# Layer 1's keys-times-values product on half of the columns, with the halves exchanged by transfers

## The chip, the cores and the metric

The kernel runs on one core of a Trainium2 chip. The metric is the device time of one execution in microseconds; the time of a version is the median of its runs. Engines are called PE (TensorE, matrix products), DVE (VectorE), ACT (ScalarE), POOL (GpSimd) and SP (SyncE, which here only issues transfers).

## The reference, cut to what matters

The program applies four layers to an array of 4 images x 512 channels x 1024 positions, all in f32: an attention of 8 heads (layer 0), a linear attention (layer 1), an attention of one head over a layer norm (layer 2), and an attention of 4 heads over a group norm (layer 3). The change is in layer 1:

```python
V = einsum('bcn,oc->bon', xf, wv) + bv          # 512 channels
V = gate * V                                    # gate: max + mean over positions
Qf, Kf = softplus(Q), softplus(K)               # 64 features each
KV = einsum('bmn,bcn->bmc', Kf, V)              # 64 x 512
norm = 1 / einsum('bnm,bm->bn', Qf, sum(Kf) + EPS)
wval = einsum('bnm,bmc,bn->bcn', Qf, KV, norm)
out = x + gamma * wval
```

The kernel never forms V. Since V is linear in x, it computes (Kf x^T) first, a 64 x 512 matrix for each image, and multiplies that by wv^T. This second product, of (64 x 512) by (512 x 512), plus bv times the sums of the keys, is the matrix `kv` that the change touches.

## The kernel before, in words

Channels lie on the 128 partitions in four chunks (`NC = 4`); positions are handled in two blocks of 512 (`NTB = 2`). Images go through each layer one after the other. Every f32 product of the source is two records of PE in the profile.

PE's instructions run in the order in which the program issues them (a manual schedule for that engine alone). The order on DVE, ACT, POOL and SP is chosen by a planner from priorities and its own estimates of times; `soon()` raises a priority.

Layer 1 of an image is cut into pieces, the list that `linear_attention` returns at its end, and these are filled into the large products of other work. `slot()` stands between those products: each call takes the next piece from the list `pieces` and issues it. For the first three images the other work is layer 0's projection of the next image (`project_qkv`): 11 slots among its first products, then 7 in `project_v`, so that 18 slots stand against 16 pieces. `flush()` issues what remains. For the last image the pieces lie among layer 2's weight products (6 slots), its first projection (7), `project_v` (7) and `one_head` (10), together with layer-norm pieces, and one more piece after them that writes the updated image to memory (`away`) and loads another (`back`). `project_v` and `one_head` are both built by `seven_products`, a scheme of seven products in place of eight, whose results DVE joins with additions (lines 746, 783, 789).

The pieces that matter here come in this order. `keys_times_x` (line 1493) forms Kf x^T in two halves of 64 rows, one from even and one from odd blocks of positions. `divide_queries` divides the query features by the norm. `transpose_kx` transposes the result, copies it from PSUM by ACT (`kxh`), and adds the two halves of 64 columns by DVE into `kxt`, once for each of two copies, so that `kxt` has 128 columns of which the second 64 repeat the first. `keys_times_values` multiplies by wv: four products (one for each chunk of channels), 128 columns wide, so that the 64 rows of the result stand twice in `kv`, on partitions 0 to 63 and 64 to 127. Both copies are needed, because `update` multiplies the lower half of the partitions with the first block of positions and the upper half with the second, side by side. The feature tile `feat` and `kv` live in one buffer, which the profile names `block`. After an empty piece (`idle`), `update(0)` and `update(1)` each fill two PSUM tiles of the pool that also holds attention's scores (two buffers), and DVE adds them to x, 128x1024 at a time (line 1558).

Small tiles of 128x512 come from `row_tile`, which has three buffers.

Of the kernel before, what the change touches and what calls it, by code (L numbers as in the profile page):

```python
# [15 lines left out]
ALU = mybir.AluOpType  # L16
# [6 lines left out]
NC = C // P  # L23
# [4 lines left out]
M = 64  # L28
# [447 lines left out]
def plain_path(ctx: ExitStack, tc: tile.TileContext, d: dict, out: bass.AP, count):  # L476
# [11 lines left out]
    nc = tc.nc  # L488
# [11 lines left out]
    def acc_tile():  # L500
        return ps_acc.tile([P, TB], F32, tag="acc", name="acc")

    def two_tile(name):
        return ps_sc.tile([P, 2, TB], F32, tag="sc", name=name)

    def row_tile(name):
        return work.tile([P, TB], F32, tag="row", bufs=3, name=name)
# [18 lines left out]
    def chunks_tile(tag, name, bufs=1):  # L526
        return work.tile([P, NC, TB], F32, tag=tag, bufs=bufs, name=name)
# [71 lines left out]
    wv1 = chunks_tile("xn", "wv1", 2)  # L599
# [8 lines left out]
    kv = block1[:, 3, :]  # L608
    bv1 = const.tile([P, C], F32, name="bv1")
# [37 lines left out]
    def product(ps, lhs, rhs):  # L647

        for c in range(NC):
            nc.tensor.matmul(ps, lhsT=lhs(c), rhs=rhs(c), start=(c == 0), stop=(c == NC - 1))  # L650
# [751 lines left out]
    def linear_attention(b, scratch):  # L1402

        x = xs[b]
        t = {}
        flat = lambda tile: tile.rearrange("p a s -> p (a s)")
        half = lambda h: slice(h * M, (h + 1) * M)
# [119 lines left out]
        def transpose_kx():  # L1527
            ps = two_tile("kxt")[:, 0, :]
            for c in range(NC):
                nc.tensor.transpose(ps[:, bass.ts(c, P)], t["kx"][:, bass.ts(c, P)], ident)  # L1530
            halves = row_tile("kxh")
            nc.scalar.copy(halves, ps)
            h = halves.rearrange("p (c a m) -> p c a m", c=NC, m=M)
            kxt = t["kxt"] = row_tile("kxt").rearrange("p (c a m) -> p c a m", c=NC, m=M)
            for a in range(2):
                nc.vector.tensor_tensor(
                    kxt[:, :, a, :], h[:, :, 0, :], h[:, :, 1, :], ALU.add
                )

        def keys_times_values():  # L1540

            ps = two_tile("kv")[:, 0, :]
            product(
                ps, lambda c: t["kxt"][:, c].rearrange("p a m -> p (a m)"), lambda c: wv1[:, c, :]
            )
            nc.vector.scalar_tensor_tensor(kv, bv1, t["kcol"], ps, ALU.mult, ALU.add)

        def update(a):

            for o in (2 * a, 2 * a + 1):  # L1550
                ps = two_tile("upd")
                for tb in range(NTB):
                    nc.tensor.matmul(  # L1553
                        ps[:, tb, :], lhsT=kv[half(tb), bass.ts(o, P)],
                        rhs=feat[half(tb), bass.ts(tb, TB)], start=True, stop=True,
                    )
                xv = x[:, o, :]
                nc.vector.scalar_tensor_tensor(
                    xv, flat(ps), t["gate"][:, o : o + 1], xv, ALU.mult, ALU.add
                )  # L1560
# [11 lines left out]
            both(lambda: keys_times_x(2), lambda: keys_times_x(3), sum_keys),  # L1572
            divide_queries,
            transpose_kx,
            keys_times_values,
            idle,
            *[lambda a=a: update(a) for a in range(NC // 2)],
        ]

# [109 lines left out]
    with tc.manual_schedule(engines={mybir.EngineType.PE}):  # L1689
# [8 lines left out]
        for b in range(B):  # L1698
            vt = v_tiles()
            if b > 0:  # L1700
                pieces.extend(linear_attention(b - 1, lambda i: vt[i]))
            q, k = project_qkv(
                wqkv0, "bqkv0", lambda tb: xs[b][:, :, bass.ts(tb, TB)], vt,
                lambda: chunks_tile("ot", "ws"), first=(b == 0),
                between=outputs_bias,
            )
            flush()
            if b > 0:
                away(b - 1)
                if b + 1 < B:  # L1710
                    nc.sync.dma_start(x_tile(b + 1), xin[b + 1])
                else:
                    back(0)
            if b == 0:
                os = output_sums(wo0)
            if b == B - 1:
                w2 = wpool.tile([P, 3 * NC, C], F32, tag="wqkv", name="w2")
                nc.sync.dma_start(w2, d["w2"].rearrange("(c p) o -> p c o", p=P))
            attention(
                b, q, lambda c, j: k[:, c, bass.ts(j, P)], vt, 8, 64.0**-0.5, wo0, os, bo0[0],  # L1720
                plain=(b == B - 1),
            )
# [31 lines left out]
        flush()  # L1754
        wo2 = load_wo(d["wo2"])
        lin = linear_attention(B - 1, lambda i: pt_tile("l1"))

        norms[1][0]()
# [4 lines left out]
        for o in range(NC):  # L1763
            ps = gps.get(o)
            if ps is None:
                ps = acc_tile()
# [5 lines left out]
        for o in range(NC):  # L1772
            ps = acc_tile()
# [11 lines left out]
        for b in range(B):  # L1785
# [9 lines left out]
            half = NC // 2  # L1795
# [156 lines left out]
```

## Time and profile before

| | before |
|---|---|
| median of 3 runs | 2435.08 us (2434.74 to 2436.24) |
| profiled execution | 2434.68 us |
| its span, first to last instruction | 2433.0 us |
| PE busy | 2416.0 us (99%) |
| DVE busy | 1497.2 us (62%) |
| ACT busy | 697.6 us (29%) |
| POOL busy | 250.8 us (10%) |
| kv products (line 650), 32 records | 592 ns median of one |
| kxt additions, 128x256, 8 | 419 ns median of one |
| kv = bv * sum + product, 128x512, 4 (line 1546) | 748 ns median of one |
| granted TensorE clock | 1.000 |

The table's times of single instructions are durations on their engine. Products on PE are pipelined: a new record of 512 columns starts long before 592 ns have passed, so that the length of a stage on PE is to be read from where it starts and where the next one starts, not from the sum of its records. The chain of waits lists the work that set the end, in order of time, and is the view for this. In lists of DVE, ACT and SP by time, the bracket at the end of a line is the idle time just before the instruction and what ended it.

### The profile page before, as it was taken

Reading aid. Unit: us, or ns where it says so; the run is one execution under the profiler, and the core shown is the slowest. Engines: PE = TensorE matmul, PEld = TensorE weight load, DVE = VectorE, ACT = ScalarE, POOL = GpSimd, SP = SyncE. Lnnn points to the kernel's source line nnn. Section 1 sums busy time; section 2 is a strip of 40 time slices with the busy share of each in tenths; the row PEclk is TensorE's granted clock in tenths of the full one; section 3 lists DMA queues with packets and bytes.
Section 4 is the critical chain, followed back from the end, with each engine's and each line's share of the span. In section 5 each row is a group of like instructions: output and inputs, shape, how many; then the busy total and the mean of one; then the engine's idle time right before and its main releaser. Section 6 shows DMA issues by size and latency. Waiting matters only on the chain.

```text
span 2433.0 us, 24544 instructions
## 1 busy us (share of the span) xinstructions
PE 2416.0 (99%) x10002; PEld 1203.5 (49%) x10002; DVE 1497.2 (62%) x1786; ACT 697.6 (29%) x860; POOL 250.8 (10%) x240
## 2 busy tenths in 40 slices
PE   9999999999999999999999999999999999999999
PEld 4444544453455344544646446455556446555653
DVE  3678577757875789556595775754453554445344
ACT  1454154406431643121211302013321330322132
POOL 4001100110020002102103021021020001002000
PEclk9999999999999999999999999999999999999999
DMA  5001120211022121111001020110110011001001
GB/s 186 9 11 42 46 79 17 55 61 44 19 77 87 58 58 53 44 52 69 1 0 69 5 87 0 52 70 18 35 70 0 18 35 52 1 35 35 1 22 45
DMA packets 41900, 104.35 MB, mean 43 GB/s; under 512 B 3419, under 2 KB 19291, under 8 KB 38838
## 3 DMA queue, kind: packets, MB, share of 16 engines
q1 hardware_dynamic: 41782, 102.73, 12.5%
q8 instruction: 80, 1.31, 0.2%
q14 instruction: 38, 0.31, 0.0%
HBM read 68.98 MB, written 33.74 MB: 42 GB/s over the span
## 4 chain that ended last, share of the span: by engine, by line
PE 98%; DVE 1%; ACT 1%; issue 0%; DMA 0%; SPq 0%; DVEq 0%
PE acc L716 19%; PE acc L841 12%; PE acc L976 9%; PE acc L991 9%; PE sc L945 9%; PE sc L940 9%; PE acc L848 8%; PE acc L1093 7%; PE acc L1325 6%; PE acc L1286 2%; PE acc L1027 1%; PE acc L650 1%; PE upd L1553 1%; PE acc L1493 1%; PE kv L650 1%; PE feat L650 1%
## 5 line engine op out<-in xcount | busy, mean ns | idle before, releaser
L950 ACT ACTIVATE pt<-sc 128x1024 f32<-128x1024 f32 x384 | 379.2, 1022 | 541.2 <-PE sc L945 304.0
L959 DVE TENSOR_TENSOR sum<-sum,pt 128x1024 f32<-128x1024 f32 x256 | 314.4, 1228 | 159.3 <-ACT pt L950 147.2
L976 PE MATMUL acc<-pt,v 64*64 64x512 f32 x2048 | 248.4, 591 | 0.0
L940 PE MATMUL sc<-q,k 64*64 64x512 f32 x2048 | 245.5, 591 | 1.1 <-ACT pt L950 1.1
L991 PE MATMUL acc<-pt,v 128*128 128x512 f32 x512 | 240.8, 594 | 0.0
L945 PE MATMUL sc<-q,k 128*128 128x512 f32 x512 | 239.8, 593 | 0.0
L716 PE MATMUL acc<-t,ws 128*128 128x512 f32 x384 | 173.9, 593 | 0.0
L704 POOL TENSOR_TENSOR ws<-wqkv 128x256 f32<-128x256 f32 (+1 forms) x40 | 39.2, 981 | 1296.7 <-PE acc L1027 516.1
L956 DVE TENSOR_TENSOR sum<-pt 128x1024 f32<-128x1024 f32 x64 | 78.0, 1219 | 137.4 <-ACT pt L950 137.4
L991 PEld LDWEIGHTS acc<-pt,v 128*128 128x128 f32 x512 | 96.6, 190 | 125.3 <-issue 121.6
L945 PEld LDWEIGHTS sc<-q,k 128*128 128x128 f32 x512 | 96.8, 190 | 116.2 <-issue 93.1
L976 PEld LDWEIGHTS acc<-pt,v 64*64 64x64 f32 x2048 | 77.5, 133 | 143.9 <-issue 141.1
L940 PEld LDWEIGHTS sc<-q,k 64*64 64x64 f32 x2048 | 76.9, 133 | 141.8 <-issue 132.9
L716 PEld LDWEIGHTS acc<-t,ws 128*128 128x128 f32 x384 | 72.7, 190 | 88.0 <-issue 87.3
L755 ACT COPY v<-acc 128x512 f32<-128x512 f32 x24 | 14.0, 585 | 305.2 <-PE acc L841 305.2
L687 DVE RECIPROCAL rd<-acc 128x512 f32<-128x512 f32 (+1 forms) x24 | 80.5, 3353 | 29.1 <-PE acc L1027 29.1
L841 PE MATMUL acc<-ws,t 128*128 128x256 f32 x384 | 86.8, 379 | 0.0
L848 PE MATMUL acc<-qs,w 128*128 128x512 f32 x192 | 86.3, 592 | 0.0
L848 PE MATMUL acc<-q,ln 128*128 128x512 f32 x192 | 85.8, 593 | 0.0
L1093 PE MATMUL acc<-ot,wo 128*128 128x256 f32 x336 | 80.6, 383 | 2.7 <-ACT ou L1112 2.7
L746 DVE TENSOR_TENSOR v<-acc,v 128x512 f32<-128x512 f32 x72 | 49.6, 690 | 53.7 <-PE acc L841 53.6
L755 ACT COPY q<-acc 128x512 f32<-128x512 f32 x40 | 23.4, 585 | 195.8 <-PE acc L716 195.8
(323 smaller groups left out, 3420.1 us busy)
## 6 DMA issues: line engine op xcount, KB each, us to landing
home<-x SPq DMA_DIRECT2D x8, 2048.0 KB
x<-home SPq DMA_DIRECT2D x8, 2048.0 KB
squares<-squares SPq DMA_DIRECT2D x32, 256.0 KB
out<-x SPq DMA_DIRECT2D x32, 256.0 KB
rds<-quotients SPq DMA_DIRECT2D x30, 256.0 KB
rds<-quotients SPq DMA_DIRECT2D x7, 1024.0 KB
x<-in_x SPq DMA_DIRECT2D x3, 2048.0 KB
v<-squares SPq DMA_DIRECT2D x12, 512.0 KB
```

The lines of the kernel that those rows point to most:

```text
L687: nc.vector.reciprocal(rd, ps)
L716: nc.tensor.matmul(ps, lhsT=w[:, m, :], rhs=x[:, m, :], start=start, stop=stop, skip_group_check=True)
L841: nc.tensor.matmul(ps[:, bass.ts(r, C // 2)], lhsT=x[:, m, bass.ts(2 * o + r, P)], rhs=w[:, m, :], start=(start and r == 0), stop=stop, sk ...
L848: nc.tensor.matmul(ps, lhsT=x[:, m, bass.ts(o, P)], rhs=w[:, m, :], start=start, stop=stop, skip_group_check=True,)
L940: nc.tensor.matmul(ps[half(h), s, :], lhsT=key(g, i)[half(s), half(h)], rhs=q[qb][half(s), g, :], start=True, stop=True,)
L945: nc.tensor.matmul(ps[:, s, :], lhsT=key(g, 2 * i + s), rhs=q[qb][:, g, :], start=True, stop=True)
L950: exps.append(nc.scalar.activation(pt, ps, AF.Exp, scale=scale).ins)
L959: adds.append(nc.vector.tensor_tensor(acc, acc, pt, ALU.add).ins)
L976: nc.tensor.matmul(outs[qb, g][r][half(s), :], lhsT=v[i // 2][half(r), i % 2, g * P + s * hd : g * P + (s + 1) * hd], rhs=pt[half(r), s, : ...
L991: nc.tensor.matmul(outs[qb, g][0], lhsT=v[j // 2][:, j % 2, bass.ts(g, P)], rhs=pt[:, s, :], start=(j == 0), stop=(j == NT - 1),)
L1093: nc.tensor.matmul(ps[i][:, bass.ts(o, n)], lhsT=w[:, m, bass.ts(o, P)], rhs=t[:, m, :], start=(start and m + o == 0), stop=(stop and m == ...
L1325: nc.tensor.matmul(ps[i, o], lhsT=w[m][:, bass.ts(o, P)], rhs=t[m], start=(start and m == 0), stop=(stop and m == 3), skip_group_check=True,)
```

## The change

`kxt` keeps one copy of 64 columns. `keys_times_values` now issues four products of 64 columns: chunks 0 and 1 of the channels accumulate into the lower half of the partitions, chunks 2 and 3 into the upper half, in alternation. Each half thus holds a partial sum over half of the channels. ACT copies both from PSUM into a tile `own`. Two transfers on SP write `own`'s upper half to the lower half of a second tile `other`, and its lower half to the upper half. DVE forms bv times the keys' sum plus `own`, and a new piece, `add_halves`, adds `other`, so that both halves of `kv` again hold the full sum. The new piece stands behind the empty one, so that the list has 17 pieces and both updates are one slot later.

```diff
-            kxt = t["kxt"] = row_tile("kxt").rearrange("p (c a m) -> p c a m", c=NC, m=M)
-            for a in range(2):
-                nc.vector.tensor_tensor(
-                    kxt[:, :, a, :], h[:, :, 0, :], h[:, :, 1, :], ALU.add
-                )
+            t["kxt"] = row_tile("kxt")[:, : NC * M].rearrange("p (c m) -> p c m", m=M)
+            nc.vector.tensor_tensor(t["kxt"], h[:, :, 0, :], h[:, :, 1, :], ALU.add)
 
         def keys_times_values():
 
             ps = two_tile("kv")[:, 0, :]
-            product(
-                ps, lambda c: t["kxt"][:, c].rearrange("p a m -> p (a m)"), lambda c: wv1[:, c, :]
-            )
-            nc.vector.scalar_tensor_tensor(kv, bv1, t["kcol"], ps, ALU.mult, ALU.add)
+            for i, h in itertools.product(range(NC // 2), range(2)):
+                c = h * NC // 2 + i
+                nc.tensor.matmul(
+                    ps[half(h), :], lhsT=t["kxt"][:, c, :], rhs=wv1[:, c, :],
+                    start=(i == 0), stop=(i == NC // 2 - 1),
+                )
+            own = row_tile("kv")
+            nc.scalar.copy(own, ps)
+            other = t["other"] = row_tile("kv")
+            for h in range(2):
+                nc.sync.dma_start(other[half(h)], own[half(1 - h)])
+            nc.vector.scalar_tensor_tensor(kv, bv1, t["kcol"], own, ALU.mult, ALU.add)
+
+        def add_halves():
+
+            nc.vector.tensor_tensor(kv, kv, t["other"], ALU.add)
...
             transpose_kx,
             keys_times_values,
             idle,
+            add_halves,
             *[lambda a=a: update(a) for a in range(NC // 2)],
```

## The prediction

> **What bounds the kernel now.** I read the busy times first, then the chain of waits over the whole run, then the same chain in two stretches around the edited stage, then VectorE's and SyncE's instructions in order of time. On the page:
>
> ```profile
> PE 2416.0 (99%) x10002; PEld 1203.5 (49%) x10002; DVE 1497.2 (62%) x1786; ACT 697.6 (29%) x860; POOL 250.8 (10%) x240
> ...
> PE 98%; DVE 1%; ACT 1%; issue 0%; DMA 0%; SPq 0%; DVEq 0%
> ```
>
> TensorE is busy 2416.0 of 2433.0 us and is 98% of the chain. So time taken off TensorE comes off the end, as long as nothing new makes TensorE wait. The chain around the edited stage of the first image (start, us, what; an f32 product is two records, so x8 is four products):
>
> ```profile
> 268.19 1.87 PE acc L1493 x8
> 270.05 3.63 PE acc L716 x8
> 273.68 1.87 PE acc L1493 x8
> ...
> 284.50 3.46 PE acc L841 x16
> 287.95 3.43 PE kv L650 x8
> 291.39 6.91 PE acc L841 x32
> 298.29 1.92 PE upd L1553 x8
> 300.21 3.65 PE acc L841 x16
> 303.86 1.92 PE upd L1553 x8
> 305.78 7.10 PE acc L841 x32
> ```
>
> The edited product (kv) takes 3.43 us between two stretches of other products without a gap. keys_times_x (L1493) has four products of the same moving size, each filling 64 columns of the array and alternating between its two halves: 1.87 us. The pieces stand one slot (x16, about 3.43 us) apart. The last image is alike:
>
> ```profile
> 1011.42 3.56 PE kv L650 x8
> 1014.98 6.91 PE acc L841 x32
> 1021.89 1.92 PE upd L1553 x8
> 1023.81 3.65 PE acc L841 x16
> 1027.46 1.92 PE upd L1553 x8
> ```
>
> **What the Trainium skill says.** "TensorEngine Tiling (Array Packing)", section Theoretical Speedup: up to 2x when the stationary operand has at most 64 columns. The trace agrees: 1.87 against 3.43 us. Its section Key Properties says that a change of tiling mode drains TensorE. The trace agrees again: from one L1493 stage to the next is 273.68 - 268.19 = 5.49 us, and the eight full-width records between are worth 3.43, so the narrow stage costs 2.06 us, against a bare half of 3.43, 1.72: about 0.35 us for both switches. "DMA: Bandwidth & Descriptors", section Anatomy of one DMA, gives about 2.0 us fixed per transfer plus bytes over 436 GB/s, fitted for another issue path; the trace has 1.77 us from the issue of a quotients transfer of 8 KB (210.54) to the issue of the read that waits for it (212.31), so the fixed part is of that order.
>
> **The change part by part.**
>
> 1. TensorE, keys_times_values. Removed: four full-width products per image, 3.43 us, and the 32 records after them take 6.91 where 4 x 1.72 = 6.88 (eights of them start at 1016.55, 1018.27 and 1020.00): 3.46 us together (last image 3.56 + 0.03 = 3.59). Added: four half-width products in the L1493 form (128 rows, 64 columns, 512 moving, different moving data in the two halves, as there), with full-width records on both sides: 2.06 us. Gain 3 x 1.40 + 1.53 = **5.7 us**. Bounds: if the two switches cost nothing, 3 x 1.74 + 1.87 = 7.1; if the halves did not overlap, -4 x 0.35 = -1.4.
>
> 2. kxt: one addition of 128x256 (0.42 us) instead of two. VectorE ended the second at 286.01, TensorE read it at 287.8: hidden in three images.
>
> 3. ACT: one copy of 128x512 from PSUM added, 0.59 us by the kxh copy. ACT is otherwise idle for 24.09 us before the attention's first exponential (beyond a 1.28 us table load). Hidden; a copy late by 1 us only makes the transfer late by 1 us.
>
> 4. The transfers: two of 64 partitions x 2 KB = 128 KB each on SP, 0.35 to 0.6 us per issue. The trace of before shows none between two places in SBUF. Low bound 1.8 us (the 8 KB one), high bound 6.3 us (the 2 MB write home, 1031.07 to 1037.39). I take 1.77 + 0.35 for the second issue + 256 KB at about 400 GB/s (0.65) = 2.8 us. SP waits for the ACT copy; behind it on SP stands only the write home of x at 307.47, which waits for the updates anyway.
>
> 5. VectorE: the scalar_tensor_tensor now reads SBUF (0.75 as before) and one addition of 0.69 us is new. Counting from the start of kv: products end at 1.9, copy 2.6, transfers 5.4, addition 6.2. The first update reads kv at 2.06 + 3 slots x 3.43 = 12.4. Cover: 6 us; even the high bound of 6.3 ends at 9.7. The addition is in VectorE's queue ahead of the joins of project_v (0.69 each, and idle 1.04 between):
>
> ```profile
> 291.43 0.75 DVE L1546 SCALAR_TENSOR_TENSOR block<-bv,kcol,kv 128x512 f32<-128x512 f32 x1 [5.41 <-PE kv L650]
> 293.15 0.69 DVE L783 TENSOR_TENSOR v<-v,acc 128x512 f32<-128x512 f32 x1 [0.98 <-PE acc L841]
> 294.88 0.69 DVE L789 TENSOR_TENSOR v<-v,acc 128x512 f32<-128x512 f32 x1 [1.04 <-PE acc L841]
> ```
>
> If it waits there for the transfer, the joins behind it are late; TensorE needs the first of them three products (5.2 us) later, so a wait under about 3 us costs nothing. I take 0; bounds 0 and 3 us an image.
>
> 6. The extra piece. Both updates come one slot later. In the first three images 18 slots take 16 pieces now and 17 after, so no remainder is run in a block; 7.10 us (two slots) between the last update and the scores become one. The scores take the two PSUM buffers that the update used; VectorE's two update additions end 3.7 us after the update's start, the scores come at 1.92 + 3.63 = 5.5: cover 1.9 us, cost 0. The next x, loaded after the write home (307.47, 313.86), comes about 2 us later and is read more than 100 us later.
>
> 7. In the last image the 20 slots before one_head are full. The second update moves into one_head, behind its first ten products: from 1027.5 to about 1029.4 - 1.5 - 2.1 + 13.8 + 3.4 = 1043. Its own price on TensorE is the same. With it goes the round trip of x:
>
> ```profile
> 1031.07 0.34 SPq L574 DMA_DIRECT2D home<-x  x1
> 1037.39 0.34 SPq L577 DMA_DIRECT2D x<-home  x1
> ...
> 1047.38 0.68 DVE L1588 TENSOR_TENSOR s<-x 128x512 f32<-128x512 f32 x1
> ```
>
> Write 6.3 us, read until about 1044.6 (DMA goes idle between 1043 and 1045): 13.5 us. After the change: updates done 1046.8, home 1053.2, back 1060.4, three additions (2.1 us). The lnsums product that reads them comes at 1077.48 - 1.5 = 1076. Cover 13 us: cost 0. Without cover: see the second rival. VectorE's additions for it now fall where joins and exponential sums keep it full (1057.7 to 1064.7 almost without a gap): 0 to 2 us, I take 0.
>
> **Sum.** -5.7 + 0 = -5.7 us. On the profiled execution: 2434.68 (span 2433.0 and 1.7 around it) becomes 2429.0. The median shown, 2435.08, is 0.40 above that execution, so I give 2429.4, -0.23%. Changes within 0.2% (4.9 us) are about what a measurement of this kernel cannot tell from none, so the forecast lies just beyond that line, at 2430.2.
>
> **Rivals.**
>
> *Part of it is given back (no measurable change).* VectorE's, ACT's and SP's orders are not written by hand; moving the updates and adding two SP transfers can reorder them. A wait of 0.3 to 1.5 us at the joins of each image, or once 2 us in one_head (part 7), leaves -1 to -4.5 us: 2430.6 to 2434. For it: the next stage, attention, has VectorE at 7 tenths of the time. Against: every join of project_v in the first image shows about 1 us of idle time before it, or 0.3 just after an update.
>
> *x comes back too late (slower).* If the three additions of s keep their place in VectorE's queue, shortly behind the second update, VectorE waits about 13.7 us there for the round trip, and one_head's joins stand behind. TensorE goes on for about four products (6.9 us) until it needs one, then waits; with the additions and the late joins that is 9 to 12 us: -5.7 + 9 to 12 = +3 to +6, 2438 to 2441. It decides when the wait in the queue passes about 7 + 5.7 us. Against: in the trace of before VectorE did two joins ahead of these additions though they were issued later in the program, as if placed by an expected arrival.
>
> *The halves do not run side by side.* +0.35 us for the switches in each image: 2436.5. Against: L1493 and the 128x64 form of features both overlap.
>
> **How the numbers follow.** Forecast 0.60 (own range 2428.0 to 2430.2), given back 0.27, no overlap 0.02, late x or another new wait above 5 us 0.11. Faster by over 0.2%: 0.60. Within: 0.27 + 0.02 = 0.29. Slower: 0.11. The range goes from the bare half (2435.08 - 7.1 = 2428.0, less 0.4 of spread) up to the end of the second case with its spread: 2427.6 to 2434.8; the slow cases lie outside.
>
> **What would show it.** Right: kv as 64-column records in about 1.9 us, next stretch longer by 0.15; the transfers landed 2 to 4 us after the copy; no TensorE wait at the updates; TensorE's busy time down by 5 to 6 us and the idle 17 us unchanged. Part 7 is wrong if TensorE stands still between 1045 and 1080. The prediction is wrong if kv takes over 3 us, or if a TensorE wait appears behind a join or at the first scores of images 1 to 3.

## The result, and the profile after

| | before | after |
|---|---|---|
| median, 18 runs each | 2435.61 us (2434.69 to 2436.85) | 2430.08 us (2429.38 to 2430.95) |
| profiled execution | 2434.68 us | 2429.38 us |
| its span | 2433.0 us | 2427.7 us |
| PE busy | 2416.0 us | 2410.6 us |

The ratio is 0.9978, with a 95% interval of 0.9971 to 0.9984: 5.5 us, or 0.23%, faster. The forecast was 5.7 us.

The first lines of the page after:

```profile
PE 2410.6 (99%) x10002; PEld 1199.1 (49%) x10002; DVE 1497.6 (62%) x1786; ACT 700.5 (29%) x864; POOL 250.7 (10%) x240
...
PE 98%; DVE 1%; ACT 1%; issue 0%; DMA 0%; SPq 0%; DVEq 0%
```

TensorE's busy time fell by 5.4 us and the span by 5.3; the shares of the chain are the same. So nothing new was put in TensorE's way. The chain around the stage, first image (start, us, what):

```profile
288.08 1.87 PE kv L1542 x8
289.95 10.56 PE acc L841 x48
300.50 1.92 PE upd L1562 x8
302.42 3.65 PE acc L841 x16
306.07 1.92 PE upd L1562 x8
307.99 3.65 PE acc L841 x16
311.64 1.06 PE sc L940 x8
```

kv's eight records take 1.87 us, as keys_times_x takes in both kernels. The scores of the kernel before, for comparison:

```profile
312.88 1.06 PE sc L940 x8
```

From kv to the first scores it is 311.64 - 288.08 = 23.56 us, and was 312.88 - 287.95 = 24.93 us: 1.37 us saved, with no wait in between. The second and third image give the same: kv starts at 520.94 and 753.79, the scores at 544.50 and 777.36. In the last image the stretch ends with the first lnsums, the product that needs x back. After the change:

```profile
1007.45 1.87 PE kv L1542 x8
...
1072.17 0.86 PE lnsums L1606 x2
```

and before, where kv starts at 1011.42:

```profile
1077.64 0.86 PE lnsums L1596 x2
```

That is 1072.17 - 1007.45 = 64.72 us instead of 1077.64 - 1011.42 = 66.22: 1.50 us. The sum is 3 x 1.37 + 1.50 = 5.6 us.

VectorE and SyncE in the same stretch (start, us, engine, line; idle time before it and its cause in the bracket):

```profile
290.61 1.16 SPq L1550 DMA_DIRECT2D kv<-kv  x2
```

```profile
290.62 0.75 DVE L1551 SCALAR_TENSOR_TENSOR block<-bv,kcol,kv 128x512 f32<-128x512 f32 x1 [4.80 <-ACT kv L1547]
291.91 0.69 DVE L783 TENSOR_TENSOR v<-v,acc 128x512 f32<-128x512 f32 x1 [0.54 <-PE acc L841]
293.64 0.69 DVE L789 TENSOR_TENSOR v<-v,acc 128x512 f32<-128x512 f32 x1 [1.04 <-PE acc L841]
294.24 0.68 DVE L1555 TENSOR_TENSOR block<-block,kv 128x512 f32<-128x512 f32 x1
```

The new addition (L1555) is done at 294.9, and the first update starts at 300.50: 5.6 us of cover remain. It starts right behind the second join (L789), without idle time before it, so that its start does not tell when the transfers were done. The trace does: their packets run from 291.78 to 293.20, and the last completion signal comes at 293.54, 2.93 us after the first issue. DMA share and GB/s are the last two numbers of a line here (the others are the length of the stretch, busy times of PE, PEld, DVE, ACT and POOL, and the granted clock):

```profile
292.00:293.00 1.00, 1.00 (x6) 0.88 (x5) 0.60 (x1) 0.00 (x0) 0.00 (x0) 1.00 0.90 197
293.00:294.00 1.00, 1.00 (x6) 0.89 (x5) 0.36 (x1) 0.00 (x0) 0.00 (x0) 1.00 0.04 10
```

### The profile page after: what moved, and what is told of

It reads as the page before. It is cut to its first block, busy times and chain, and to the rows that moved or that the text cites. A ratio compares the mean times of both kernels' runs of the same rounds, so it can differ in the third digit from the quotient of the medians.

```text
span 2427.7 us, 24564 instructions
## 1 busy us (share of the span) xinstructions
PE 2410.6 (99%) x10002; PEld 1199.1 (49%) x10002; DVE 1497.6 (62%) x1786; ACT 700.5 (29%) x864; POOL 250.7 (10%) x240
## 4 chain that ended last, share of the span: by engine, by line
PE 98%; DVE 1%; ACT 1%; issue 0%; DMA 0%; SPq 0%; DVEq 0%
PE acc L716 19%; PE acc L841 12%; PE acc L976 9%; PE acc L991 9%; PE sc L945 9%; PE sc L940 9%; PE acc L848 8%; PE acc L1093 7%; PE acc L1325 6%; PE acc L1286 2%; PE acc L1027 1%; PE acc L650 1%; PE upd L1562 1%; PE acc L1493 1%; PE feat L650 1%; PE feat L1417 0%
## 5 line engine op out<-in xcount | busy, mean ns | idle before, releaser
L746 DVE TENSOR_TENSOR v<-acc,v 128x512 f32<-128x512 f32 x72 | 49.6, 689 | 53.2 <-PE acc L841 53.2
```

## The experiments

The medians of the kernel before in the three groups of experiments were 2435.79 (the first four), 2435.64 (the next three) and 2435.52 us (the last two). Profiled executions differ by up to 1.4 us in the first 20 us, where TensorE's opening products wait for loads (the next stretch starts at 20.11 us after the change, at 21.49 in one experiment). So I compare stages inside each execution, and medians for the whole.

### The shift of the updates by itself

```diff
             keys_times_values,
+            idle,
             idle,
```

> The kernel before with one more empty piece ahead of the two updates, so that only the shift of the updates by a slot is tried. Theory (the gain is TensorE time in the kv stage, the shift is hidden): kv stage stays 3.43 us, time within 0.5 us of the kernel before, although in the last image the second update and the round trip of x come about 14 us later. Rival (the shift itself moves the time, by new orders on the other engines or by a late x): 2 us or more to either side; the rival that x returns too late says +3 to +6.

This edit is made to the kernel before; the others are made to the changed kernel. Measured 2435.83 us against 2435.79; ratio 0.9999 (0.9991 to 1.0007). From kv to the scores it is 24.93 us (288.74 to 313.67), exactly as before. The last image's second update starts at 1045.40 instead of 1027.46 and the write home of x at 1049.02 instead of 1031.07, but the chain has no wait:

```profile
1045.40 1.92 PE upd L1553 x8
1047.32 31.10 PE acc L848 x72
1078.42 0.86 PE lnsums L1597 x2
```

So the extra slot neither costs nor brings anything; the gain is in the rest of the change.

### The addition in the place of the empty piece

```diff
             keys_times_values,
-            idle,
             add_halves,
```

> The changed kernel with the addition of the halves in the place of the empty piece, so that both updates keep the slots they had before the change. Theory: 5.5 us under the kernel before, within 0.5 us of the changed kernel; the update follows kv's start by about 8.9 us, the transfers land by 6.7 and the addition ends by 7.4, so still no TensorE wait. Rival (the transfers need the extra slot as cover): TensorE waits at the first update, 0.5 us or more an image, 2 us or more in all.

Measured 2430.61 us, ratio 0.9978 (0.9970 to 0.9987): the changed kernel's. The first update starts 8.98 us after kv (298.43 and 289.45), again without a wait. The extra slot was not needed.

### No cover for the transfers

```diff
-            keys_times_values,
-            idle,
-            add_halves,
+            both(keys_times_values, add_halves),
```

> The changed kernel with the product and the addition of the halves in one piece and no empty piece behind it, so that the first update comes one slot after kv. Theory (the transfers cost nothing only while other products cover them): the update would follow kv's start by 5.5 us, but the sum is there at about 6.9 (three images) to 7.4 us (the last): TensorE waits 1.4 to 2 us at each first update, 6 to 8 us in all, so the time comes back to within 1.5 us of the kernel before or 1 to 2 us above it. Rival (the transfers are faster than the place of the addition in VectorE's queue suggests, about 2.8 us as forecast): waits of 0.7 us an image, 3 us in all, and a time 2.5 us under the kernel before.

Measured 2436.25 us, ratio 1.0001 (0.9993 to 1.0009): the whole gain is gone. The chain shows who is waited for:

```profile
288.87 1.87 PE kv L1542 x8
290.73 3.67 PE acc L841 x16
294.40 0.02 issue
294.42 0.03 DVE v L789
294.46 0.57 issue
295.03 0.69 DVE block L1555
...
295.86 1.99 PE upd L1562 x8
```

The update comes 6.99 us after kv in the first image and in the last one (1019.86 and 1012.87), 1.45 us later than it could (1.87 + 3.67). Four such waits are 5.8 us, and the median is 6.2 us above the changed kernel's. So 3.67 us of other products do not cover the exchange and the addition behind it; 7.10 us did, in the run before this one.

The wait is not all the transfers' own. TensorE waits for the addition (L1555), and the addition stands behind a join (L789) in VectorE's queue:

```profile
294.42 0.69 DVE L789 TENSOR_TENSOR v<-v,acc 128x512 f32<-128x512 f32 x1 [1.04 <-PE acc L841]
295.03 0.68 DVE L1555 TENSOR_TENSOR block<-block,kv 128x512 f32<-128x512 f32 x1
```

The first transfer is issued at 291.39 and the last completion signal comes at 294.32, after 2.93 us (2.90 to 2.93 in the four images), just before the join starts. In the changed kernel's last image, the only one where the addition waited for the transfers themselves, it began 0.12 us after the last signal. By that, it could have begun here at about 294.44 instead of 295.03. So I estimate that about 0.6 of the 1.45 us are owed to the place in VectorE's queue and the other 0.85 to the transfers; no run with the addition ahead of the join was made. The rival in the expectation, with waits of 0.7 us an image, was right on the length of the transfers (about 2.8 us) and had left out the join.

### The transfers taken away

```diff
-            other = t["other"] = row_tile("kv")
-            for h in range(2):
-                nc.sync.dma_start(other[half(h)], own[half(1 - h)])
+            t["other"] = own
```

> The changed kernel without the two transfers: the new addition adds each half's own partial sum once more, so the sums over the other half of the channels are left out of kv. Theory (the exchange is hidden): within 0.5 us of the changed kernel, kv stage 1.87 us. Rival (the transfers cost something, on SP or by VectorE's wait): 1 us or more under the changed kernel.

This kernel leaves out the sums over the other half of the channels. Measured 2429.93 us (2430.08 with the transfers); ratio to the kernel before 0.9977 (0.9969 to 0.9986). From kv to the scores it is 23.57 us (288.02 to 311.59), and from kv to the first lnsums of the last image 64.72 (1007.39 to 1072.11), both as with the transfers. TensorE pays nothing for them in the changed kernel.

### Both halves of the work in one half of the array

```diff
-            for i, h in itertools.product(range(NC // 2), range(2)):
-                c = h * NC // 2 + i
+            for c in range(NC):
                 nc.tensor.matmul(
-                    ps[half(h), :], lhsT=t["kxt"][:, c, :], rhs=wv1[:, c, :],
+                    ps[half(0), :], lhsT=t["kxt"][:, c, :], rhs=wv1[:, c, :],
...
+            for h in range(2):
+                nc.scalar.copy(own[half(h)], ps[half(0), :])
```

> The changed kernel with all four narrow products (64 columns) accumulating in the lower half of the array's columns; ACT then copies that half of PSUM to both halves of the tile, so no transfers are needed and the new addition is empty. Nothing is left out. Only the pairing of the two halves is undone. Theory (the gain is products running side by side in the two halves): kv stage 3.4 to 3.6 us with one switch in it, so 1.75 us an image, 7 us in all, over the changed kernel, that is 1 to 2 us over the kernel before. Rival (a product with 64 columns of weights is faster by itself, since its weight loads are 0.13 instead of 0.19 us): kv stage 1.87 us, same time as the changed kernel.

The rest of this edit takes out the transfers and the addition, which the run before showed to be hidden. Measured 2436.99 us, ratio 1.0005 (0.9997 to 1.0014), 6.9 us above the changed kernel. In the chain:

```profile
288.75 3.58 PE kv L1541 x8
292.33 10.56 PE acc L841 x48
```

Eight narrow records in one half take 3.58 us: eight times 0.43, plus about 0.15. A narrow product is no faster than a wide one by itself. The gain is two of them side by side, and without that the stage is 0.15 us longer than before, by the switch at its start; the stretch behind it has the other switch (10.56 us, and 10.36 for the same 48 records in the run with the shift alone). From kv to the scores it is 25.27 us (288.75 to 314.02), 0.34 more than before the change.

### Another order of the four products

```diff
-            for i, h in itertools.product(range(NC // 2), range(2)):
+            for h, i in itertools.product(range(2), range(NC // 2)):
```

> The changed kernel with the four products in another order: both of the lower half, then both of the upper half, in place of alternation; the same work. Theory (the gain is the overlap of products in different halves of the array, which a queue in order can only give to neighbours): kv stage about 3.0 to 3.4 us instead of 1.87, only the two products in the middle overlap, so 4 to 6 us over the changed kernel. Rival (the overlap does not depend on the order, or the gain comes from lighter weight loads): kv stage 1.87 us, same time as the changed kernel.

Measured 2430.22 us, ratio 0.9976 (0.9966 to 0.9986). The kv stage stays at 1.87 us: my expectation was wrong. Weight loads show how the products went (start, us, engine, form; x is the number of loads merged):

```profile
288.30 0.20 PEld L1542 LDWEIGHTS kv<-wv,kxt 128*64 128x64 f32 x4 [0.33 <-issue]
288.79 0.15 PEld L1542 LDWEIGHTS kv<-wv,kxt 128*64 128x64 f32 x2 [0.28 <-issue]
289.21 0.15 PEld L1542 LDWEIGHTS kv<-wv,kxt 128*64 128x64 f32 x2 [0.28 <-issue]
```

Four loads at once, then two and two, as with alternation, though here the upper half's first record stands behind four records of the lower half. TensorE took it ahead of those: in the order of issue the upper half could have begun only with the lower half's last record, 3 x 0.43 us later, and the stage could not have ended in 1.87 us. So the order in which the program issues products is not kept between the two halves. How far this reaches was the next question.

### keys_times_x in one piece, in alternation and in turn

First both pieces of keys_times_x were merged into the second one's slot:

```diff
-            both(lambda: keys_times_x(0), lambda: keys_times_x(1)),
-            both(lambda: keys_times_x(2), lambda: keys_times_x(3), sum_keys),
+            idle,
+            both(*[lambda i=i: keys_times_x(i) for i in range(NT // 2)], sum_keys),
```

> The changed kernel with both keys_times_x pieces in one: an empty piece first, then all eight narrow products and the sum of the keys in the second slot. Nothing is left out; one pair of switches between full and narrow columns an image goes. Theory (two switches cost 0.35 us): the narrow stage is 3.6 us long for sixteen records, and the time is 4 x 0.35 = 1.4 us under the changed kernel. Rival (the extra 0.35 us is a property of the first products of a stage, such as waiting for their operands): same time as the changed kernel.

Measured 2428.93 us, ratio 0.9972 (0.9961 to 0.9982), 1.15 us under the changed kernel. The stage is 3.58 us:

```profile
272.74 3.58 PE acc L1493 x16
```

In the changed kernel both narrow stages and the eight wide records between them took from 268.31 to 275.68, 7.37 us; less 3.43 for those records and 3.58, that is 0.36 us for the pair of switches that went. So a stage's switches do cost 0.35 us, and this kernel is the fastest of all that ran.

Then the same eight products, the lower half's four ahead of the upper half's four:

```diff
-            for s in range(2):
...
+            for s, i in itertools.product(range(2), range(n)):
                 nc.tensor.matmul(
```

> The kernel with merged keys_times_x pieces, its eight products in another order: the four of the lower half first, then the four of the upper half. With four products the order made no difference, against the expectation. Theory A (TensorE takes products of the free half ahead of ones that wait for the busy half, at least eight records deep): narrow stage 3.6 us as with alternation, same time. Theory B (it reaches only a few records ahead): narrow stage 4.5 to 7 us, 4 to 14 us over the kernel with merged pieces in alternation.

Measured 2435.91 us, ratio 1.0001 (0.9993 to 1.0009): 7.0 us lost on the order alone.

```profile
271.79 5.35 PE acc L1493 x16
```

The 5.35 us fit (8 + 4) x 0.43 + 0.19: the upper half starts four records late, so four pairs run together and the last four run alone. The weight loads confirm it:

```profile
273.06 0.14 PEld L1493 LDWEIGHTS acc<-v,kf 128*64 128x64 f32 x1 [0.29 <-issue]
273.49 0.19 PEld L1493 LDWEIGHTS acc<-v,kf 128*64 128x64 f32 x3 [0.29 <-issue]
273.92 0.19 PEld L1493 LDWEIGHTS acc<-v,kf 128*64 128x64 f32 x2 [0.23 <-issue]
274.35 0.19 PEld L1493 LDWEIGHTS acc<-v,kf 128*64 128x64 f32 x2 [0.23 <-issue]
274.83 0.14 PEld L1493 LDWEIGHTS acc<-v,kf 128*64 128x64 f32 x1 [0.29 <-issue]
```

They come one by one up to 273.06, for the lower half alone. At 273.49 the lower half's fifth record starts, so that four of its eight are still to be done, and with it the upper half's first. Then loads come in pairs, and from 274.83 one by one again, for the rest of the upper half. A reach of that kind also explains the order that made no difference, where only four records stood ahead. Four records (two f32 products) fit both runs; with other sizes of product it was not tried.

### x late by five slots

```diff
-            *[lambda a=a: update(a) for a in range(NC // 2)],
+            lambda: update(0),
+            *[idle] * (5 if b == B - 1 else 0),
+            lambda: update(1),
```

> The changed kernel with five more empty pieces ahead of the last image's second update, so that this update, the write home of that image and the load of the next come five slots (17 us) later. In the changed kernel x is back at about 1056 and the first product that needs its sums starts at 1072. Theory (the round trip has about 13 us of cover and no more): TensorE waits 2 to 6 us at the lnsums product or just ahead of it, and the time is 2 to 6 us over the changed kernel. Rival (the planner moves the sums of x anyway and something else covers it): within 0.5 us. Rival (x late blocks VectorE's joins): 9 us or more.

Measured 2438.07 us, ratio 1.0010 (1.0004 to 1.0017), 8.0 us above the changed kernel, more than the 2 to 6 expected. The chain:

```profile
1073.25 0.02 issue
1073.28 0.69 DVE pts L746
...
1075.20 1.23 DVE acc L1249
1076.43 0.61 DVE s L1600
...
1077.79 0.70 DVE s L1602
...
1078.63 2.04 PE lnsums L1608 x2
1080.67 7.49 PE acc L1286 x16
```

TensorE stands still for 5.4 us (1073.25 to 1078.63). Then the lnsums records take 2.04 instead of 0.86 us and the next sixteen 7.49 instead of 6.87: 1.8 us more. Together these are 7.2 of the 8.0 us; the rest stays open (the first 20 us alone vary by up to 1.4 us). The granted clock (the third number from the end, a mean over each window) shows why the records after the wait are longer:

```profile
1078.00:1081.00 3.00, 2.37 (x3) 1.17 (x4) 0.77 (x2) 0.00 (x0) 0.00 (x0) 0.56 0.00 0
1081.00:1085.00 4.00, 4.00 (x10) 1.67 (x9) 3.79 (x7) 3.01 (x5) 0.00 (x0) 0.90 0.00 0
```

The means come from one drop: from 1078.39, near the end of the wait, to 1081.80 the trace has a clock of 0.50, for 3.41 us, and a whole one before and after. Half of 3.41 is 1.7 us, about the time lost. The last completion signal of x's read comes at 1075.72, 2.5 us after TensorE stopped. VectorE's additions of x (L1600, L1602) follow at 1076.4, behind joins and exponential sums (L746, L1249) that were not held up by x. So a late x can hurt here, but five slots later than in the changed kernel, and the joins were not blocked.

## Why the prediction was right, point by point

- **TensorE in the kv stage (step 1).** Forecast 3 x 1.40 + 1.53 = 5.7 us, measured 3 x 1.37 + 1.50 = 5.6 us. The price of 2.06 us for a narrow stage, taken from the distance between two keys_times_x stages, held: 1.87 in the stage and 0.20 in the stretch behind it (10.56 us for the 48 records, and 10.36 in the run with the shift alone). Undoing the pairing cost 6.9 us, so this term is shown, not only argued. That run was 1.5 us above the kernel before, where the prediction had put 1.4 us for halves that do not overlap.
- **kxt and ACT's copy (steps 2 and 3).** The copy (0.59 us, 290.00) runs right behind the products, and the scores are no later for it. Hidden, as forecast.
- **The transfers (step 4).** Forecast 2.8 us, measured 2.93, 2.93 and 2.92 us from the first issue to the last completion signal in three images. The sum was right in part by luck, since its terms were not: the second issue began 0.56 us after the first, not 0.35; the packets of both, with that gap in them, ran for 1.41 us (197 GB/s in the line shown above), where 0.65 us at 400 GB/s had been taken; and the rest was 1.5 us (1.17 before the first packet, 0.34 behind the last) instead of 1.77. In the last image it took 4.09 us, and the addition waited 0.49 us for it (1009.97 to 1014.18 from issue to addition). All lie inside the bounds of 1.8 to 6.3 us.
- **The cover (step 5).** The addition was to end 6.2 us after kv's start and ended at 6.84. It was expected in VectorE's queue ahead of the joins of project_v; it came behind two of them (291.91 and 293.64). In the first image that cost it an estimated 0.6 us (it began at 294.24; the last signal came at 293.54, and 0.12 us are needed after it), and TensorE nothing. The update came at 12.42, forecast 12.4. The cover was 5.6 instead of 6 us; the run without cover shows that it was needed.
- **The extra slot (step 6).** Cost 0 forecast; the shift alone measured 0.04 us between medians. The scores come 5.57 us after the last update's start, forecast 5.5, and VectorE has freed the buffers at 309.65, 3.6 us after it, forecast 3.7.
- **x in the last image (step 7).** Cost 0, as forecast. The second update came at 1039.15 instead of about 1043, because I had not taken off the 4.1 us saved in the first three images. The same error was in the place where x is needed (1076 forecast, 1072.17 measured), so the two cancel. The cover was still less than forecast: the additions of x ended at 1061.77, which leaves 10.4 us and not 13, because the read took longer (last signal at 1057.55) and the additions stood behind joins.
- **The rivals.** Nothing was given back by new orders on other engines. The late x did not occur: VectorE had the additions of x at 1059.16, behind the joins. Forced five slots later, x did cost time, but by TensorE's own wait and the clock after it, not by blocked joins.

## What to carry to other kernels

Products with 64 columns are worth pairing where TensorE sets the end: two in different halves of the columns take the time of one (f32, 512 columns of moving data here), with 0.35 us to pay for the two switches of a stage, so group such stages and alternate the halves in the program. An exchange between partitions for it was free behind 7.10 us of other products and not behind 3.67; measure the distance from the product to its reader before choosing the slot. Where a reader starts right behind another instruction of its engine, its start is no measure of the transfer: look for the transfer's completion. Price a narrow stage by the distance between two known stages, which contains the switches, and not by its own length.

## What the runs showed of the hardware that was not expected

- TensorE paired products of different halves although they stood one half after the other in the program, as long as four records stood ahead (kv stage 1.87 us in both orders). With eight ahead, half of the pairing was lost (5.35 against 3.58 us).
- A wait of 5.4 us on TensorE cost 1.8 us more behind it, at a granted clock of 0.50 for 3.41 us.
- Two transfers of 128 KB within SBUF were complete 2.9 us after the first issue, 1.16 us of it for issuing both. In the last image they took 4.09 us. There a packet of 16 KB of the queue that the page calls "instruction" began 1.24 us after the first issue and ran for 1.28 us. In each of the six runs with such a packet inside the exchange, the last image took 3.7 to 4.5 us; without one, in the run without cover, 2.90. That the packet is the cause is likely, but not tested by itself.
